# A three-stage perceiver kernel on one core: identity products ahead of the first rows, W transposed on TensorE, and four smaller moves

## The chip, the cores and the metric

The kernel runs on one core of one Trainium2 chip. The metric is the device time of an execution in microseconds (us), lower is better. A profiled execution gives, beside its own time, a trace of every engine: TensorE (PE; its weight loads are listed apart as PEld), VectorE (DVE), ScalarE (ACT), GpSimd (POOL) and SyncE (SP), which here only starts DMAs.

## What is computed

Three residual stages on x, 8 x 64 tokens of width 512, all in float32. The first stage attends over a context of 8 x 1601 rows; its matrix W is used twice, once on the queries and once, transposed, on the result:

```python
def _L0_xattn_ref(proj_p, proj_q, W, b):
    trans_q = jnp.einsum('bqh,oh->bqo', proj_q, W) + b
    att_weights = jnp.einsum('bph,bqh->bpq', proj_p, trans_q)
    att_norm = jax.nn.softmax(att_weights, axis=-1)
    att_vec = jnp.einsum('bpq,bqh->bph', att_norm, proj_q)
    return jax.nn.relu(jnp.einsum('bph,oh->bpo', att_vec, W) + b)

x = x + _L0_xattn_ref(_layernorm(x, axis=-1), ctx_1024, L0_xattn_W, L0_xattn_b)
x = x + _L0_attn_ref(_layernorm(x, axis=-1), ...)
x = x + _L0_ffn_ref(_layernorm(x, axis=-1), ...)
```

The second stage is a transformer block with causal linear attention of 16 heads (features elu(x proj) + 1) and a gelu MLP of width 2048. The third is a mixture of 8 experts (gated MLPs of width 1024), of which each token takes its best 2.

## The kernel before

The 512 tokens are NT = 4 tiles of 128, and 512 columns are KC = 4 chunks of 128. Every engine executes its instructions in the order in which the program writes them; nothing is rearranged.

**Start.** SP loads x and W (w_sb, L113), then everything else in one list (`stream`, `order`, `issue_to`): context keys (ctxT), context rows (ctx), the small inputs and the later weights. Large items go into a ring of RING = 12 buffers, and an item is started only when the buffer that it will take has been read. A second copy of W, transposed on the host (xw_t), is in that list behind the first context rows and lands in w_t. On POOL five areas inside v_sb are cleared first (L122); small vectors are loaded into every 32nd row of them later. Then the identity (ident) and other constants are made.

The rows of x are normalized by VectorE and ACT, two tiles at a time, and turned by `turn_p` (4 PE transposes and one ACT copy per tile). The queries times W, `pw_half`, are made in 2 halves of the tokens x 4 chunks; each is 4 accumulated matmuls of 256 columns. An f32 matmul is two records in the trace, a transpose is one.

**Context stage.** For each tile t, `key_group(t, g)` makes scores for a quarter g of the keys, `softmax` and `turn_scores` follow, `weigh(t, g)` multiplies by a third g of the rows, `turn_av` and `attended` multiply by w_t. `add_and_normalize(t)` is a chain of VectorE and ACT steps over the result, which ends in hn; `turn_h(t)` turns hn with 4 PE transposes and 4 VectorE steps into h_t; and `values(t, n)` multiplies h_t by half n of wv. For the last tile the order on PE is values(2, 0), values(2, 1), turn_h(3), values(3, 0), values(3, 1).

**Linear attention.** Eight pairs of heads j pass through `linear`, `features`, `products` and `attend_j`; the last step of `attend_j(j)` is a VectorE chain that ends in a_t. `output(t, js)` accumulates the output products of tile t over j. After `attend_j(7)`, PE has output(2) for j = 0 to 3, and then the j = 6 and 7 of tiles 0 and 1, the second of which needs the last a_t. `join` and `normal` follow on VectorE and ACT, and `turn_h2` on PE.

**Router and experts.** After the MLP the tokens are ranked by expert; "counts" is a small matmul into a bank of the tag "mm", read by VectorE. The PSUM pool is then closed and a new one (pse) opened. `whole_tile` runs an expert on 128 gathered tokens: up products, gating, transposes, and `down` into one bank y of 128x512. `add_rows` scales y and adds it to the output in DRAM by an indirect DMA. For the last expert's tile ACT scales the left half of y and VectorE the right one.

PSUM has 8 banks of 128x512 f32; in the first pool four have the tag "mm" (`mm_bank`) and four "acc" (`acc_bank`).

Of the kernel before, what the change touches and what calls it, by code (L numbers as in the profile page):

```python
# [32 lines left out]
NE, FE = 8, 1024  # L33
NQ = 4
FQ = FE // NQ
R = P // NQ
REST = 3 * R
# [3 lines left out]
NBIG = 7  # L41
LN_EPS = 1e-5
RING = 12
AHEAD = 6


@with_exitstack
def perceiver_kernel(
# [5 lines left out]
    context_tail: bass.AP,  # L54
    context_last: bass.AP,
    xw: bass.AP,
    xw_t: bass.AP,
    xb: bass.AP,
    wq: bass.AP,
    wk: bass.AP,  # L60
# [11 lines left out]
    nc = tc.nc  # L72
# [11 lines left out]
    def mm_bank(name):  # L84
        return ps.tile([P, 512], F32, tag="mm", name=name)
# [21 lines left out]
    h_t = la.tile([P, KC, B * S], F32, name="h_t")  # L107
# [10 lines left out]
    half = H * DH // 2  # L118
    last_in = [v_sb[:, 2, :half], v_sb[:, 2, half:], v_sb[:, 3, half:], v_sb[:, 1, half:]]
    xb_in = v_sb[:, 0, :D]  # L120
    for rows in [xb_in, *last_in]:
        nc.gpsimd.memset(rows, 0.0)  # L122
    col = const.tile([P, COLS], F32, name="col")

    streamed, order, issued = {}, [], [0]
# [2 lines left out]
    def stream(key, src):  # L128
        order.append((key, src))
# [20 lines left out]
        stream_keys(1, g)  # L150
    for t in range(NT):
        stream_rows(t, 0)
        if t == 0:
            stream("xw_t", xw_t)
        stream_keys(t + 1, 2)
        stream_rows(t, 1)
        stream_keys(t + 1, 3)
        stream_rows(t, 2)
        stream(("tail", t), context_tail[t])
        for g in range(2):  # L160
            stream_keys(t + 2, g)
        if t == NT - 2:
            for n in range(2):
                stream(("wv", n), wv[n])
# [16 lines left out]
    places_of = {"xb": xb_in[0:P:32, :], "col": col, "xw_t": w_t}  # L181
    places_of.update({("last", t): last_in[t][0:P:32, :] for t in range(NT)})

    def in_ring(key):
# [36 lines left out]

    ident = const.tile([P, P], F32, name="ident")
    make_identity(nc, ident)
    eps = const.tile([P, 1], F32, name="eps")
    nc.gpsimd.memset(eps, LN_EPS)
    warm0 = const.tile([P, 1], F32, name="warm0")
# [140 lines left out]
    def turn_p(t):  # L367
        bank = mm_bank(f"tr_p_{t}")
        for c in range(KC):
            nc.tensor.transpose(bank[:, c * P : (c + 1) * P], pn[:, t, c * P : (c + 1) * P], ident)  # L370
        nc.scalar.copy(p_t[:, :, t * P : (t + 1) * P], bank.rearrange("p (c q) -> p c q", c=KC))
# [4 lines left out]
    def pw_half(half, hc):  # L376
        cols = slice(half * 2 * P, (half + 1) * 2 * P)
        bank = mm_bank(f"pw_{half}_{hc}")
        for oc in range(KC):
            nc.tensor.matmul(  # L380
                bank[:, : 2 * P],
                w_sb[:, oc, hc * P : (hc + 1) * P],
                p_t[:, oc, cols],
                start=(oc == 0),
                stop=(oc == KC - 1),
            )
        nc.scalar.copy(pw_t[:, hc, cols], bank[:, : 2 * P])
# [3 lines left out]
    for t in range(0, NT, 2):  # L391
        of = [statistics(xs[:, t + h, :], f"p_{t + h}") for h in range(2)]
        for h in range(2):
            normalize(pn[:, t + h, :], xs[:, t + h, :], *of[h], f"p_{t + h}")
        if t == 0:
            turn_p(0)
            turn_p(1)
    pw_half(0, 0)
    pw_half(0, 1)
    turn_p(2)  # L400
    turn_p(3)
    pw_half(0, 2)
# [146 lines left out]
    def turn_h(t):  # L549
        bank = mm_bank(f"tr_h_{t}")  # L550
        for c in range(KC):
            nc.tensor.transpose(bank[:, c * P : (c + 1) * P], hns[t][:, c * P : (c + 1) * P], ident)
        for c in range(KC):
            nc.vector.tensor_scalar(  # L554
                h_t[:, c, t * P : (t + 1) * P],
                bank[:, c * P : (c + 1) * P],
                g1_c[:, c : c + 1],
                beta1_c[:, c : c + 1],
                ALU.mult,
                ALU.add,  # L560
            )

    def values(t, n):
        wv_n = need("wv", n)
        bank = mm_bank(f"v_{n}_{t}")
        for c in range(KC):
            nc.tensor.matmul(  # L567
                bank, h_t[:, c, t * P : (t + 1) * P], wv_n[:, c, :], start=(c == 0), stop=(c == KC - 1)
            )
        nc.scalar.copy(v_sb[:, t, n * 512 : (n + 1) * 512], bank)  # L570
# [49 lines left out]
            values(t - 2, 1)  # L620
        attended(t)
    add_and_normalize(NT - 1)
    for n in range(2):
        values(NT - 2, n)
    turn_h(NT - 1)
    for n in range(2):
        values(NT - 1, n)
    done(("wv", 0), ("wv", 1))
# [6 lines left out]
    if True:  # L635
        a_t = la1.tile([P, H * DH // P, B * S], F32, name="a_t")

        nj = H * DH // P
# [115 lines left out]
        def output(t, js):  # L754
            if t not in wo_banks:
                wo_banks[t] = (mm_bank if t < 2 else acc_bank)(f"wo_{t}")
            for j in js:
                nc.tensor.matmul(  # L758
                    wo_banks[t],
                    a_t[:, j, t * P : (t + 1) * P],  # L760
                    wo_r[j // 4][:, j % 4, :],
                    start=(j == 0),
                    stop=(j == nj - 1),
                )
# [8 lines left out]
        products(nj - 1)  # L773
        output(1, range(nj - 2))
        attend_j(nj - 1)
        output(2, range(nj // 2))
        for t in range(2):
            output(t, [nj - 2, nj - 1])

# [34 lines left out]
        of = join(0), join(1)  # L814
        for t in range(2):
            normal(t, *of[t])
        output(2, range(nj // 2, nj))
        of = join(2)
        output(3, range(nj // 2))
        normal(2, *of)  # L820
# [234 lines left out]
    t = NT - 1  # L1055
# [85 lines left out]
    if True:  # L1141
# [5 lines left out]
        def y_bank(side, name):  # L1147
            return pse.tile([P, 512], F32, tag=f"y{side}", name=name)
# [64 lines left out]
        def add_rows(key, y, n, side, by_vector=False):  # L1213

            _, dst, gate = slots[key]
            y_sb = moe2.tile([P, D], F32, tag=f"ysb{side}", bufs=2 - side, name=f"y_sb_{key[0]}_{key[1]}")
            if key == (NE - 1, 0):
                nc.scalar.activation(y_sb[:n, : D // 2], y[:n, : D // 2], AF.Copy, scale=gate[:n, :])
                nc.vector.tensor_scalar(y_sb[:n, D // 2 :], y[:n, D // 2 :], gate[:n, :], None, ALU.mult)
            elif by_vector:  # L1220
                nc.vector.tensor_scalar(y_sb[:n, :], y[:n, :], gate[:n, :], None, ALU.mult)
            else:
                nc.scalar.activation(y_sb[:n, :], y[:n, :], AF.Copy, scale=gate[:n, :])  # L1223
            nc.gpsimd.indirect_dma_start(  # L1224
                out=out,
                out_offset=bass.IndirectOffsetOnAxis(ap=dst[:n, :], axis=0),
                in_=y_sb[:n, :],
                in_offset=None,
                bounds_check=B * S + P - 1,
                oob_is_err=True,  # L1230
                compute_op=ALU.add,
            )

        def whole_tile(key, up_of, down_of, between=lambda k: None, side=0):


            nm = f"{key[0]}_{key[1]}"
            xg_t = turned[key]

            def up(q):  # L1240
                bank = side_bank(side, f"up_{nm}_{q}")
                for c in range(KC):
                    nc.tensor.matmul(  # L1243
                        bank, xg_t[c], up_of[q][:, c, :], start=(c == 0), stop=(c == KC - 1)
                    )
                return gated(side, bank, f"{nm}_{q}")

            def down(q, h_t):
                w = down_of[q // 2]
                for j in range(2):  # L1250
                    nc.tensor.matmul(  # L1251
                        y, h_t[:, j, :], w[:, 2 * (q % 2) + j, :], start=(q + j == 0), stop=(q + j == NQ)
                    )
# [12 lines left out]
            between(1)  # L1266
            h_t3 = hidden_t(side, hid3, f"{nm}_3")
            down(2, h_t2)
            between(2)
            down(3, h_t3)  # L1270
            add_rows(key, y, P, side)

        def group(e, up_of, down_of):


            nm = f"{e}_1"
# [5 lines left out]
            hid, h_t = [], {}  # L1282
# [7 lines left out]
            for h in range(2):  # L1290

                bank = side_bank(1, f"up_{nm}_1") if h else y_bank(1, f"up_{nm}_0")
                for c in range(KC):
# [3 lines left out]
                    for q in range(NQ):  # L1297
# [4 lines left out]
                            start=(c == 0),  # L1302
# [33 lines left out]
            add_rows((e, 1), y, R, 1)  # L1336

        def three_groups(e, up_of, down_of):

            nm = f"{e}_1"  # L1340
# [69 lines left out]
            add_rows((e, 1), y, REST, 1, by_vector=True)  # L1410

        if True:

# [225 lines left out]
    "ctx_tail",  # L1639
    "ctx_last",  # L1640
    "L0_xattn_W",
    "L0_xattn_W_T",
    "L0_xattn_b",
    "L0_attn_wq",
    "L0_attn_wk",
# [82 lines left out]
```

## Time and profile before

| what | us | from |
|---|---|---|
| median of 3 runs (650.0 to 650.8) | 650.71 | times |
| the profiled execution | 647.66 | times |
| its span, first to last instruction | 645.5 | page, head |
| first PE instruction | 7.45 | PE's timeline |
| start of the scores | 28.0 | chain of waits |
| last context rows weighed, tile 3 | 150.5 | chain of waits |
| last of v | 177.4 | chain of waits |
| start of the MLP's hidden products | 285.9 | PE's timeline |
| first expert product | 409.1 | PE's timeline |
| last y is scaled | 637.8 | timeline |

The page divides the span into 40 slices of 16.1 us. Its row for the DMA queues reads:

```profile
GB/s 345 405 414 422 423 425 421 427 426 422 193 80 47 86 2 131 1 131 0 130 52 79 70 96 95 134 95 348 114 375 54 200 206 338 173 367 188 274 18 16
```

The first ten numbers are the start and the context stage; after them the loads have room. In the lists of waits a row names the instruction that waited, its line, what it waited for, the total, how often and the longest. In a timeline a row has its start, its length, engine, line, operation, result <- operands, the shape and the number of instructions merged; in brackets stands the idle time before it and what ended that. Rows of PE overlap a little, because the end of a matmul is modelled.

### The profile page before, as it was taken

To read this page: it belongs to the slowest core of one execution; us is meant where nothing else is said; L and a number is where in the kernel's file an instruction comes from. 1 tells how busy PE (TensorE), PEld (TensorE's weight loads), DVE (VectorE), ACT (ScalarE), POOL (GpSimd) and SP (SyncE) were. 2 spreads that over 40 slices of the span, in tenths; PEclk is the share of its full clock that TensorE was granted. 3 is DMA by queue.
4 is the path that set the end of the run, shared out by engine and by line. 5 is a ranking of instruction groups with operands and counts; after the bars stand their busy time and mean duration, and the time that the engine had idled before them with its cause. 6 is when DMAs were issued, how large, how long until landed. Compare 5 with 4: busy or idle time off the path is not lost.

```text
span 645.5 us, 7558 instructions
## 1 busy us (share of the span) xinstructions
PE 620.4 (96%) x2956; PEld 292.7 (45%) x2956; DVE 185.5 (29%) x450; ACT 127.8 (20%) x245; POOL 64.6 (10%) x87
## 2 busy tenths in 40 slices
PE   4999999999999999999999999999999999999994
PEld 3743434344444444455444447544443344444441
DVE  5011333332316888660000035511311211011100
ACT  2241222220132123031101211311111111111110
POOL 4000000000000000050000002250102012103000
PEclk9999999999999999999999999999999999999998
DMA  8999999999421203030312222339392549496611
GB/s 345 405 414 422 423 425 421 427 426 422 193 80 47 86 2 131 1 131 0 130 52 79 70 96 95 134 95 348 114 375 54 200 206 338 173 367 188 274 18 16
DMA packets 23755, 132.70 MB, mean 206 GB/s; under 512 B 4084, under 2 KB 4084, under 8 KB 12184
## 3 DMA queue, kind: packets, MB, share of 16 engines
q1 hardware_dynamic: 19352, 123.37, 48.0%
q0 software_dynamic: 3248, 7.58, 5.3%
q10 hardware_dynamic: 1104, 1.07, 0.5%
q8 instruction: 33, 0.54, 0.3%
q14 instruction: 18, 0.15, 0.1%
HBM read 127.10 MB, written 4.91 MB: 204 GB/s over the span
## 4 chain that ended last, share of the span: by engine, by line
PE 50%; DMA 23%; issue 22%; DVE 2%; POOL 1%; POOLq 1%; ACT 0%; SPq 0%; ACTq 0%
DMA out_dram<-y_sb,dst_late 11%; DMA ctx<-in_ctx_dram 11%; PE hid L839 8%; PE mlp L860 8%; PE wk L647 4%; PE wq L647 4%; PE v L567 4%; PE wo L758 4%; PE sc L442 3%; PE av L503 3%; PE pw L380 3%; PE pr_wq L663 1%; PE xo L537 1%; PE qk L689 1%; POOL xg L1166 1%
## 5 line engine op out<-in xcount | busy, mean ns | idle before, releaser
L1243 PE MATMUL up<-e_up,xgT 128*128 128x512 f32 x224 | 100.2, 595 | 2.3 <-PEq L1569 1.4
L1243 PEld LDWEIGHTS up<-e_up,xgT 128*128 128x128 f32 x224 | 40.9, 190 | 49.9 <-issue 48.1
L1251 PE MATMUL y<-e_wo,hidT 128*128 128x512 f32 x128 | 60.8, 598 | 0.0
L839 PE MATMUL hid<-v_sb,w 128*128 128x512 f32 (+2 forms) x144 | 56.6, 545 | 0.0
L1202 DVE TENSOR_TENSOR mid<-up,act 128x256 f32<-128x256 f32 x35 | 14.9, 425 | 132.0 <-ACT act L1200 132.0
L860 PE MATMUL mlp<-w,hid_sb 128*128 128x512 f32 x112 | 51.0, 597 | 0.0
L503 PE MATMUL av<-ctx,eT 128*64 128x512 f32 x192 | 46.6, 597 | 0.7 <-DMA ctx<-in_ctx_dram 0.6
L442 PE MATMUL sc<-ctxT,pw_t 128*64 128x401 f32 (+1 forms) x256 | 46.2, 501 | 0.0
L839 PEld LDWEIGHTS hid<-v_sb,w 128*128 128x128 f32 x144 | 26.2, 190 | 29.1 <-issue 27.3
L1224 POOL DMA_INDIRECT out_dram<-y_sb,dst_late x12 | 18.3, 1524 | 174.3 <-ACT y_sb L1223 55.7
L1200 ACT ACTIVATE act<-up 128x256 f32<-128x256 f32 x35 | 13.4, 384 | 107.2 <-PE up L1243 97.4
L854 POOL TENSOR_TENSOR xin<-xin,b_bc 128x512 f32<-128x512 f32 x4 | 5.1, 1265 | 272.6 <-DVE rstd_h L796 268.4
L1251 PEld LDWEIGHTS y<-e_wo,hidT 128*128 128x128 f32 x128 | 22.5, 190 | 19.9 <-issue 19.6
L860 PEld LDWEIGHTS mlp<-w,hid_sb 128*128 128x128 f32 x112 | 20.7, 190 | 23.5 <-issue 23.4
L442 PEld LDWEIGHTS sc<-ctxT,pw_t 128*64 128x64 f32 x256 | 19.5, 136 | 25.6 <-issue 24.3
L758 PE MATMUL wo<-wo,a_t 128*128 128x512 f32 x64 | 29.1, 600 | 0.5 <-DVE a_t L734 0.5
L647 PE MATMUL wk<-h_t,wk 128*128 128x512 f32 x64 | 29.5, 604 | 0.0
L647 PE MATMUL wq<-h_t,wq 128*128 128x512 f32 x64 | 29.4, 602 | 0.0
L567 PE MATMUL v<-wv,h_t 128*128 128x512 f32 x64 | 28.7, 596 | 0.6 <-DVE h_t L554 0.6
L908 DVE TENSOR_TENSOR xs<-mlp,xs 128x512 f32<-128x512 f32 x3 | 2.1, 692 | 86.6 <-PE mlp L860 86.6
L732 DVE RECIPROCAL rden<-rden 128x512 f32<-128x512 f32 x8 | 26.8, 3353 | 0.3
L503 PEld LDWEIGHTS av<-ctx,eT 128*64 128x64 f32 x192 | 13.7, 136 | 26.8 <-issue 23.2
(266 smaller groups left out, 651.4 us busy)
## 6 DMA issues: line engine op xcount, KB each, us to landing
e_up<-in_L_ffn_up_dram SPq DMA_DIRECT2D x32, 1024.0 KB, 8.0
ctx<-in_ctx_dram SPq DMA_DIRECT2D x24, 1024.0 KB, 17.2
ctxT<-in_ctx_T_dram SPq DMA_DIRECT2D x24, 802.0 KB, 14.8
e_wo<-in_L_ffn_wo_dram SPq DMA_DIRECT2D x16, 1024.0 KB, 9.6
w<-in_L_attn_w_dram SPq DMA_DIRECT2D x8, 1024.0 KB, 4.7
ctxT<-in_ctx_T_dram SPq DMA_DIRECT2D x8, 796.0 KB, 17.5
wv<-in_L_attn_wv_dram SPq DMA_DIRECT2D x2, 1024.0 KB, 16.6
wq<-in_L_attn_wq_dram SPq DMA_DIRECT2D x2, 1024.0 KB, 17.8
```

The source lines that it names most:

```text
L380: nc.tensor.matmul(bank[:, : 2 * P], w_sb[:, oc, hc * P : (hc + 1) * P], p_t[:, oc, cols], start=(oc == 0), stop=(oc == KC - 1),)
L442: nc.tensor.matmul(sc[h * S : (h + 1) * S, :width], pw_t[:, c, (2 * t + h) * S : (2 * t + h + 1) * S], keys[h][:, c, :], start=(c == 0), s ...
L503: nc.tensor.matmul(av[h * S : (h + 1) * S, :], e_t[:, 4 * g + j, h * S : (h + 1) * S], rows[h][:, j, :], start=(g == 0 and j == 0), stop=F ...
L567: nc.tensor.matmul(bank, h_t[:, c, t * P : (t + 1) * P], wv_n[:, c, :], start=(c == 0), stop=(c == KC - 1))
L647: nc.tensor.matmul(bank, w[:, c, (j % 4) * P : (j % 4 + 1) * P], h_t[:, c, :], start=(c == 0), stop=(c == KC - 1),)
L732: nc.vector.reciprocal(rden, rden)
L758: nc.tensor.matmul(wo_banks[t], a_t[:, j, t * P : (t + 1) * P], wo_r[j // 4][:, j % 4, :], start=(j == 0), stop=(j == nj - 1),)
L839: nc.tensor.matmul(hid_banks[f][:, tokens], w[:, c, (f % 4) * P : (f % 4 + 1) * P], h2_t[:, c, tokens], start=(c == 0), stop=(c == KC - 1),)
L860: nc.tensor.matmul(acc[t], hid[:, t * P : (t + 1) * P], need("w2", f // 4)[:, f % 4, :], start=(f == 0), stop=(f == FF // P - 1),)
L1224: nc.gpsimd.indirect_dma_start(out=out, out_offset=bass.IndirectOffsetOnAxis(ap=dst[:n, :], axis=0), in_=y_sb[:n, :], in_offset=None, boun ...
L1243: nc.tensor.matmul(bank, xg_t[c], up_of[q][:, c, :], start=(c == 0), stop=(c == KC - 1))
L1251: nc.tensor.matmul(y, h_t[:, j, :], w[:, 2 * (q % 2) + j, :], start=(q + j == 0), stop=(q + j == NQ))
```

## The change

Six edits, in the order of the program:

1. The load of xw_t and the host's transpose are gone. The five clears on POOL move behind the identity.
2. NIDLE = 12 products of the identity with itself go to PE as soon as the identity is there, into a bank of the tag "acc" which nobody reads.
3. After the first two `turn_p`, PE turns W itself with 16 transposes of 128x128 into four "acc" banks; VectorE copies these to w_t, behind the first normalizations and ahead of the shuffle of xb.
4. `turn_h(3)` is issued inside values(2, 1), ahead of its last matmul.
5. output(2) takes j = 4 ahead of the last products of tiles 0 and 1 instead of behind them.
6. "counts" takes an "acc" bank. The last tile's y becomes two banks, each with 256 columns used; `down` makes its two matmuls for one bank and then for the other, and ACT and VectorE each read one.

```diff
+NIDLE = 12
...
-    for rows in [xb_in, *last_in]:
-        nc.gpsimd.memset(rows, 0.0)
...
-        if t == 0:
-            stream("xw_t", xw_t)
...
     make_identity(nc, ident)
+
+    idle_bank = acc_bank("idle")
+    for _ in range(NIDLE):
+        nc.tensor.matmul(idle_bank[:, :P], ident, ident, start=True, stop=True)
+    for rows in [xb_in, *last_in]:
+        nc.gpsimd.memset(rows, 0.0)
...
             turn_p(0)
             turn_p(1)
+
+            w_banks = [acc_bank(f"w_t_{hc}") for hc in range(KC)]
+            for hc in range(KC):
+                for oc in range(KC):
+                    nc.tensor.transpose(
+                        w_banks[hc][:, oc * P : (oc + 1) * P], w_sb[:, oc, hc * P : (hc + 1) * P], ident
+                    )
     pw_half(0, 0)
     pw_half(0, 1)
+    for hc in range(KC):
+        nc.vector.tensor_copy(w_t[:, hc, :], w_banks[hc])
...
-    def values(t, n):
+    def values(t, n, among=lambda: None):
...
         for c in range(KC):
+            if c == KC - 1:
+                among()
...
-    for n in range(2):
-        values(NT - 2, n)
-    turn_h(NT - 1)
+    values(NT - 2, 0)
+    values(NT - 2, 1, lambda: turn_h(NT - 1))
...
-        output(2, range(nj // 2))
+        output(2, range(nj // 2 + 1))
...
-        output(2, range(nj // 2, nj))
+        output(2, range(nj // 2 + 1, nj))
...
-    bank = mm_bank("counts")
+
+    bank = acc_bank("counts")
...
-            if key == (NE - 1, 0):
-                nc.scalar.activation(y_sb[:n, : D // 2], y[:n, : D // 2], AF.Copy, scale=gate[:n, :])
-                nc.vector.tensor_scalar(y_sb[:n, D // 2 :], y[:n, D // 2 :], gate[:n, :], None, ALU.mult)
+            if len(y) == 2:
+                nc.scalar.activation(y_sb[:n, : D // 2], y[0][:n, : D // 2], AF.Copy, scale=gate[:n, :])
+                nc.vector.tensor_scalar(y_sb[:n, D // 2 :], y[1][:n, : D // 2], gate[:n, :], None, ALU.mult)
...
+                width = D // len(y)
+                for n, bank in enumerate(y):
+                    for j in range(2):
+                        nc.tensor.matmul(
+                            bank[:, :width],
+                            h_t[:, j, :],
+                            w[:, 2 * (q % 2) + j, n * width : (n + 1) * width],
...
-            y = y_bank(side, f"y_{nm}")
+            y = [y_bank(side, f"y_{nm}")]
+            if key == (NE - 1, 0):
+
+                y.append(y_bank("w", f"y_{nm}_1"))
...
-    inputs["L0_xattn_W_T"] = _np.asarray(inputs["L0_xattn_W"]).T
```

More of the change, by code (lines that the diff above doesn't have):

```diff
@@ L56, in perceiver_kernel @@
     xw: bass.AP,
-    xw_t: bass.AP,
     xb: bass.AP,
@@ L179, in perceiver_kernel @@
     place = {key: i for i, (key, _) in enumerate(order)}
-    places_of = {"xb": xb_in[0:P:32, :], "col": col, "xw_t": w_t}
+    places_of = {"xb": xb_in[0:P:32, :], "col": col}
     places_of.update({("last", t): last_in[t][0:P:32, :] for t in range(NT)})
@@ L1216, in add_rows @@
             y_sb = moe2.tile([P, D], F32, tag=f"ysb{side}", bufs=2 - side, name=f"y_sb_{key[0]}_{key[1]}")
-            if key == (NE - 1, 0):
-                nc.scalar.activation(y_sb[:n, : D // 2], y[:n, : D // 2], AF.Copy, scale=gate[:n, :])
-                nc.vector.tensor_scalar(y_sb[:n, D // 2 :], y[:n, D // 2 :], gate[:n, :], None, ALU.mult)
+            if len(y) == 2:
+                nc.scalar.activation(y_sb[:n, : D // 2], y[0][:n, : D // 2], AF.Copy, scale=gate[:n, :])
+                nc.vector.tensor_scalar(y_sb[:n, D // 2 :], y[1][:n, : D // 2], gate[:n, :], None, ALU.mult)
             elif by_vector:
+                (y,) = y
                 nc.vector.tensor_scalar(y_sb[:n, :], y[:n, :], gate[:n, :], None, ALU.mult)
             else:
+                (y,) = y
                 nc.scalar.activation(y_sb[:n, :], y[:n, :], AF.Copy, scale=gate[:n, :])
@@ L1249, in down @@
                 w = down_of[q // 2]
[L1250 to L1253, printed above, removed]
+                width = D // len(y)
[5 more added lines that the diff above has]
+                            w[:, 2 * (q % 2) + j, n * width : (n + 1) * width],
+                            start=(q + j == 0),
+                            stop=(q + j == NQ),
+                        )
             hid0 = up(0)
@@ L1335, in group @@
                 )
-            add_rows((e, 1), y, R, 1)
+            add_rows((e, 1), [y], R, 1)
         def three_groups(e, up_of, down_of):
@@ L1409, in three_groups @@
                 folded(g, n)
-            add_rows((e, 1), y, REST, 1, by_vector=True)
+            add_rows((e, 1), [y], REST, 1, by_vector=True)
         if True:
@@ L1641 @@
     "L0_xattn_W",
-    "L0_xattn_W_T",
     "L0_xattn_b",
@@ L1705, in by_cols @@
         return _np.asarray(w).reshape(KC, P, -1, 512).transpose(2, 1, 0, 3)
-    for name in ("L0_xattn_W", "L0_xattn_W_T"):
-        inputs[name] = by_rows(inputs[name])[0]
+    inputs["L0_xattn_W"] = by_rows(inputs["L0_xattn_W"])[0]
     for name in ("L0_attn_wq", "L0_attn_wk", "L0_attn_wv", "L0_attn_w1"):
```

## The prediction

> **What bounds the kernel now.** I read the busy shares first, then TensorE's waits, then its timeline at the few places where it stands still. The page's first row says that TensorE (PE) is the kernel:
>
> ```profile
> PE 620.4 (96%) x2956; PEld 292.7 (45%) x2956; DVE 185.5 (29%) x450; ACT 127.8 (20%) x245; POOL 64.6 (10%) x87
> ```
>
> A change pays only where PE stands still or runs slowly. The list of PE's waits (total us, times, longest) names the places:
>
> ```profile
> PE tr_p L370 <- DVE rstd_p L362: 7.4, 1, 7.4
> ...
> PE pw L380 <- ACT h_t L371: 0.7, 1, 0.7
> PE v L567 <- DVE h_t L554: 0.6, 1, 0.6
> PE av L503 <- DMA ctx<-in_ctx_dram: 0.6, 2, 0.3
> PE wo L758 <- DVE a_t L734: 0.5, 1, 0.5
> ```
>
> Four of these are touched by the change. What the list can't show is slow work, so PE's timeline of the first 28 us comes next (start, us, instruction):
>
> ```profile
> 7.45 1.94 PE L370 MATMUL tr_p<-ident,xin 128*128 128x128 f32 x8 [7.45 <-DVE rstd_p L362]
> 10.06 6.72 PE L380 MATMUL pw<-h_t,w_sb 128*128 128x256 f32 x16 [0.68 <-ACT h_t L371]
> 16.62 1.04 PE L370 MATMUL tr_p<-ident,xin 128*128 128x128 f32 x8
> 17.49 10.53 PE L380 MATMUL pw<-h_t,w_sb 128*128 128x256 f32 x48
> ```
>
> The same products take 0.42 us each at first and 0.216 later (the chain of waits has 10.36 us for the 48); the transposes fall from 0.22 to 0.109 (0.87 for 8). PE works at half rate until about 16.3, though the granted clock reads 1.00 throughout: that column doesn't show this gate.
>
> Last, the DMA of the context stage, from the table of windows (the last columns are granted clock, DMA share, GB/s) and PE's timeline:
>
> ```profile
> 31.00:32.00 1.00, 1.00 (x8) 0.43 (x6) 0.00 (x0) 0.54 (x1) 0.00 (x0) 1.00 1.14 376
> 32.00:33.00 1.00, 1.00 (x8) 0.43 (x6) 0.00 (x0) 0.00 (x0) 0.00 (x0) 1.00 0.84 232
> ...
> 90.34 3.65 PE L503 MATMUL av<-ctx,eT 128*64 128x512 f32 x14 [0.29 <-DMA ctx<-in_ctx_dram]
> ...
> 121.25 3.65 PE L503 MATMUL av<-ctx,eT 128*64 128x512 f32 x14 [0.29 <-DMA ctx<-in_ctx_dram]
> ```
>
> From 34 to 160 us the queues move 419 to 427 GB/s without a dip, and PE stops for 0.29 us at the same point of each round, 30.9 us apart. DMA's round is 30.9 and PE's 30.6: **DMA sets the pace until 121 us**, with PE just behind. After that PE sets it. So what PE gains before 28 us survives only as far as DMA gains too.
>
> **The first rows.** The row clears (five memsets, 0.81 to 3.18) now follow the identity, which took 0.56 us on POOL (3.14 to 3.70): it is ready at 1.37 instead of 3.70, and the clears end at 3.74. POOL's sum is unchanged, so everything behind them keeps its time. The load of xb waits for its clear, up to 0.56 us longer, and on SP six key loads stand behind it; the queues then hold some 3.0 MB (x, W, two key blocks, less what moved), 7 us of work, so nothing runs dry.
>
> The 12 identity products are plain f32 products, two records each: 24 x 0.215 = 5.2 us at half rate, about 1.45 to 6.65, before the first normalized rows at 7.45: free. If weight load and product did not overlap they would cost some 0.4 each (the shortest record is 379 ns), 9.6 us, and PE would reach the first transposes at 11.05, 3.6 late. The transposes of 7.45 have the same size and run 0.22 apart; I take 5.2.
>
> What they buy is the open gate. The row: in this trace it opened 8.9 us after the first transpose, 6.2 after the first product. [...]
>
> With an open gate: transposes of rows 0 and 1, 8 x 0.109, end at 8.32. W itself is the new wait: issued at 1.74, 7.1 us to landing, 8.84. Its 16 transposes run 8.9 to 10.65 (1.74), which covers the two ACT copies that cost 0.68. Then 16 x 0.216 = 3.46, 0.87 for rows 2 and 3 (normalized at 11.64), 48 x 0.216 = 10.37: the scores start at 25.35 instead of 28.02, **2.67 earlier**. Four copies of W's banks (0.69 each, the row of o_sb) stand on VectorE ahead of the bias sums, which end at about 18.5 instead of 15.9 and are read at 28 or later; w_t is first read at 70.8. Free, with 2.8 us at stake if that cover were gone.
>
> **The removed load.** 1,024 KB at 424 GB/s is 2.47 us less for everything behind it, from the second key blocks of tile 1 on. The dip above is the queue running dry because the ring waited for the first score group (30.89): 48 + 192 KB short, 0.57 us. Freed 2.7 earlier, it doesn't occur. DMA gains 3.04; PE's own path gains 2.67 + 0.71 (its three waits: 0.13 between 55 and 60, where the windows show it busy for 4.87 of 5.00, and 0.29 twice) = 3.38. The later one counts: **3.04** in this execution. The dip belongs to a late gate, and other executions may have opened it sooner, so for the median I take 2.8 (between 2.47 and 3.04).
>
> **v's last transposes.** They now precede the last two records of values(2, 1), 0.86 us of cover for a wait of 0.59. VectorE ends hn at 168.12, the transposes would start at 168.29: 0.17 to spare, at worst 0.1 lost. The four VectorE steps and ACT's copy keep their order. **0.59**.
>
> **The output product.** PE ends at 271.08 and a_t comes at 271.63. Two records (0.86) cover it: **0.55**. VectorE's joins start 0.31 later, and one product fewer stands before turn_h2(0), at 280.5 instead of 281.2; normal(1) ends at 278.8. Nothing is late.
>
> **The counts bank.** counts and the first up product have the same bank (0 in the program's list of allocations); VectorE read it until 409.03 and up(0) began at 409.13 after 0.51 of idling. Even if all of it goes, the gathered rows xg of expert 0's rest land at 429.50 whatever PE does (PE's weight load already waits 0.17 for them), so up to 0.5 becomes a wait there. **0**, at most 0.1.
>
> **The last tile's two banks.** Twice the records at half the width, 0.216 each, with 0.19 weight loads under them as in the pw rows: free. The tail now:
>
> ```profile
> 636.80 0.47 ACT L1218 ACTIVATE y_sb<-y,xg 128x256 f32<-128x256 f32 x1 [3.01 <-PE y L1251]
> 637.31 0.48 DVE L1219 TENSOR_SCALAR y_sb<-y,xg 128x256 f32<-128x256 f32 x1 [4.93 <-ACT y_sb L1218]
> 638.07 1.55 POOL L1224 DMA_INDIRECT out_dram<-y_sb,dst_late  x1 [20.76 <-DVE y_sb L1219]
> ```
>
> VectorE waits for ACT. With its own bank ready 0.86 before the end, ACT finishes under PE and VectorE starts at 636.80: **0.51**.
>
> **Sum.** 2.8 + 0.59 + 0.55 + 0 + 0.51 = 4.45 us (4.7 against the profiled 647.66, whose span is 645.5). The runs' median is 650.71, 3 us above the profiled one, with no stage to pin it on; I carry the difference over: 650.71 - 4.45 = **646.3**.
>
> **Rivals.**
> - *The gate opens only after W.* At half rate row transposes end at 9.39 and W's at 12.83, 2.8 later than pw starts now. Opening at 16.3, 8 products run slow and scores start at 29.3, 1.25 late. PE then leads: 1.25 - 0.71 - 1.65 (the three later gains) = -1.1: **649.6**. [...] Against: 5.2 us of products come first.
> [...]
> - *The identity products overrun* to 11.05, gate open: scores at 28.35, 0.33 late; -0.38 - 1.65 = **648.7**.
> - *The load's removal is not the gain:* if PE reached 28 us no earlier, DMA's 2.47 would yield only PE's 0.71.
>
> **How the numbers follow.** Forecast 0.62 (own range 645.2 to 647.3); gate after W 0.16; its worst 0.12; overrun 0.06; something not seen 0.04. A measurement of this kernel tells about 0.2%, 1.3 us, from no change. Faster: 0.62 + 0.06 + a third of the late gate + 0.01 = 0.74. Same: 0.11 of the late gate and 0.05 of its worst, 0.16. Slower: 0.10. The range, 645.0 to 650.4, leaves out the worst case and the tails.
>
> **What would show it.** Right: tr_p records 0.109 apart at 7.45, W's transposes ending near 10.7, scores near 25.4, no dip at 32, the third-rows wait at the first tile about 3 us earlier, no waits at v and wo, VectorE's last step at PE's end. Wrong: pw records 0.42 apart, a first transpose after 7.6, or PE gaps in the rounds longer than 0.4.

## The result, and the profile after

| | us | from |
|---|---|---|
| before, median of 6 runs (649.2 to 651.2) beside the changed kernel | 650.36 | times |
| after, median of 6 runs (645.3 to 646.2) | 646.0 | times |
| ratio | 0.9925, 95% interval 0.991 to 0.9941 | times |
| profiled execution of after, and its span | 646.23, 644.5 | times, page |

The total came out as forecast, 646.0 against 646.3. Several of its terms were wrong, which is what the rest of this text is about. A caution first: the profiled execution of before (647.66) lies below all six runs that stood beside after, and that of after is the slowest of its six. The two spans differ by 1.0 us, the medians by 4.4, so the two traces are compared stage by stage and not by their ends.

PE's timeline of the first 28 us after (start, us, instruction, in brackets the idle time before it):

```profile
1.44 5.49 PE L223 MATMUL idle<-ident 128*128 128x128 f32 x24 [1.44 <-POOL ident masks.py:199]
7.61 1.43 PE L372 MATMUL tr_p<-ident,xin 128*128 128x128 f32 x8 [0.67 <-DVE xin L365]
8.87 1.95 PE L404 MATMUL w_t<-ident,w_sb 128*128 128x128 f32 x16
10.65 3.62 PE L382 MATMUL pw<-h_t,w_sb 128*128 128x256 f32 x16
...
25.44 4.94 PE L453 MATMUL sc<-ctxT,pw_t 128*64 128x401 f32 x28
```

Nearly to the tenth the front that was forecast: products done before the first rows, W's transposes at full rate until 10.65, the first 16 pw records in 3.62 instead of 6.72, scores at 25.44 instead of 28.0. The first transpose of x comes at 7.61, just past the 7.6 that was named as a sign of being wrong, because VectorE's rows came late (PE stood idle for 0.67 before it); it cost nothing, since W's transposes still start at 8.87, earlier than in the six later traces that have the full-size products or idle_turns' transposes ahead of them (8.96 to 9.14). But PE's waits for the context rows, which were to stay under 0.4, grew (the same timeline, later):

```profile
57.46 3.65 PE L514 MATMUL av<-ctx,eT 128*64 128x512 f32 x14 [0.66 <-DMA ctx<-in_ctx_dram]
...
88.98 3.65 PE L514 MATMUL av<-ctx,eT 128*64 128x512 f32 x14 [0.93 <-DMA ctx<-in_ctx_dram]
...
119.83 3.65 PE L514 MATMUL av<-ctx,eT 128*64 128x512 f32 x14 [0.25 <-DMA ctx<-in_ctx_dram]
```

The third-rows restart of tile 2, at 121.25 before, stands at 119.83: of the 2.5 us gained at the scores only 1.4 is left, and the waits for DMA took the rest. A dip of the queues is a part of why. The table of windows after (length, busy time of PE, PEld, DVE, ACT and POOL, then granted clock, DMA share, GB/s):

```profile
24.00:26.00 2.00, 2.00 (x11) 1.32 (x12) 0.00 (x0) 0.56 (x2) 0.00 (x0) 1.00 1.00 338
26.00:28.00 2.00, 2.00 (x14) 0.86 (x12) 0.00 (x0) 0.00 (x0) 0.00 (x0) 1.00 1.01 363
28.00:30.00 2.00, 2.00 (x16) 0.83 (x12) 0.00 (x0) 0.60 (x1) 0.00 (x0) 1.00 0.98 324
30.00:32.00 2.00, 2.00 (x16) 0.83 (x14) 0.00 (x0) 0.60 (x1) 0.00 (x0) 1.00 1.00 388
```

The dip at 32 is gone, and a deeper one stands at 24 to 30 (the same windows of before have 373, 417 and 412). Summing GB/s by time up to 44 us, the queues had moved 16,908 KB before and 16,718 after, so some 0.45 us of the 2.47 that the removed load saved was given back. That would leave 2.0; where the other 0.6 went is not shown.

At the other end the two y banks do what was meant, and nothing comes of it (timeline of all engines):

```profile
634.94 0.47 ACT L1231 ACTIVATE y_sb<-y,xg 128x256 f32<-128x256 f32 x1 [2.17 <-PE y L1268]
635.80 0.48 DVE L1232 TENSOR_SCALAR y_sb<-y,xg 128x256 f32<-128x256 f32 x1 [4.45 <-PE y L1268]
637.06 1.55 POOL L1239 DMA_INDIRECT out_dram<-y_sb,dst_late  x1 [20.79 <-DVE y_sb L1232]
```

ACT's half is done early and VectorE starts when PE ends. But the scatter starts 0.78 us after VectorE's end (635.80 + 0.48), where it took 0.28 before. From the first product of the last expert to the scatter there are 23.06 us (614.00 to 637.06), and 23.03 before.

### The profile page after: what moved, and what is told of

Same layout as the page of the kernel before. It is cut to its first block, busy times and chain, and to the rows that moved or that the text cites. A ratio compares the mean times of both kernels' runs of the same rounds, so it can differ in the third digit from the quotient of the medians.

```text
span 644.5 us, 7676 instructions
## 1 busy us (share of the span) xinstructions
PE 623.7 (97%) x3012; PEld 299.9 (47%) x3012; DVE 187.8 (29%) x454; ACT 127.8 (20%) x245; POOL 64.1 (10%) x87
## 5 line engine op out<-in xcount | busy, mean ns | idle before, releaser
L1268 PE MATMUL y<-e_wo,hidT 128*128 128x512 f32 (+1 forms) x144 | 60.8, 550 | 0.0
L1268 PEld LDWEIGHTS y<-e_wo,hidT 128*128 128x128 f32 x144 | 25.5, 190 | 18.2 <-issue 17.2
```

Of the source, the lines that this page charges most:

```text
L1268: nc.tensor.matmul(bank[:, :width], h_t[:, j, :], w[:, 2 * (q % 2) + j, n * width : (n + 1) * width], start=(q + j == 0), stop=(q + j == NQ),)
```

## The experiments

The theory after the result: the first three edits are worth what DMA gains, PE's start being hidden, and the later edits are worth their PE gaps. The rivals: the open gate is the gain; the new tail costs what it saves; a part of the time lies elsewhere. All kernels compute the whole output. Each ratio is to runs of before on the same chip; these had medians of 648.3, 648.0 and, for the last kernel, 651.0, so ratios are compared and not times.

### before_again: before once more

> The kernel before, unchanged, for a second trace. Its profiled execution was 647.66 us, while its other executions have a median of 650.4. [...] Theory B (the difference lies behind the context stage): the start is as before within 0.3 us, and PE shows more idle time at places without a releaser ('issue', 'PEq') in the expert stage. A time near 650 with the same PE timeline up to 409 us speaks for B.

647.57 us, one run. Scores at 27.70, third rows of tile 2 at 121.15, first expert product at 409.01: within 0.3 us of the first trace of before in each stage. So the stage marks of before can be relied on to some 0.3 us until the experts. The chip was one on which before's median is 648.3 and not 650, so whether the 3 us lie behind the context stage was not decided.

### no_idle: after without the identity products

```diff
-NIDLE = 12
+NIDLE = 0
```

> The changed kernel without its 12 identity products; W is still turned on TensorE and not loaded. [...] If the removed load carries the front alone (rival): within 0.7 us of the changed kernel.

644.45 us, 0.9943 (0.993 to 0.9956). The expectation failed: the products were to open the gate and carry the front with it, and without them the kernel still gains, some 0.2% less than after_again below. PE's timeline shows the first surprise:

```profile
7.28 1.94 PE L372 MATMUL tr_p<-ident,xin 128*128 128x128 f32 x8 [7.28 <-DVE rstd_p L364]
9.01 2.71 PE L404 MATMUL w_t<-ident,w_sb 128*128 128x128 f32 x16
11.56 3.62 PE L382 MATMUL pw<-h_t,w_sb 128*128 128x256 f32 x16
```

W's 16 transposes took 2.71 us: at 0.22 and 0.109 us each that is 7 or 8 slow ones, then fast ones. The gate opened at about 10.7, 3.4 us after the first transpose and ahead of any product. (best_no_idle, the other kernel without the products, opened it 4.9 us after its first transpose.) **It opened with nothing but transposes run.** The scores start at 26.34, only 0.9 later than after, and by the third rows that is gone: 118.65, the earliest of all. Up to the first expert product (404.87) this kernel is 1.2 us *ahead* of after. So where does it lose? The second surprise is in the first expert:

```profile
428.03 1.02 PE L1322 MATMUL up<-e_up,xgT 128*32 128x256 f32 x10 [0.44 <-PEq L1594]
430.51 2.79 PE L1322 MATMUL up<-e_up,xgT 128*32 128x256 f32 x46 [1.46 <-issue]
```

Ten products after a branch (PEq, L1594) PE stands for 1.46 us with nothing in the profile to wait for. In after the 56 products are one row (of 3.60 us; 3.23 in after_again). This was followed up last, with best_tiny.

### keep_load: identity products, but W's transpose loaded as before

```diff
+            stream("xw_t", xw_t)
...
-            w_banks = [acc_bank(f"w_t_{hc}") for hc in range(KC)]
...
-        nc.vector.tensor_copy(w_t[:, hc, :], w_banks[hc])
```

> The changed kernel with the transposed W loaded from DRAM as before, and not turned on TensorE; the identity products stay. If DMA sets the pace of the context stage (the prediction): scores start near 24.0, but the third rows of each tile come when the DMA has them, the waits there grow to 1 to 2 us, and the gain of the front is 0.6 to 1.3 us instead of 2.8: about 647.5 to 648.5, 1.5 to 2.2 us slower than the changed kernel. If the gate alone carries the front (rival): as fast as the changed kernel or 1 us faster.

646.49 us, 0.9968 (0.9956 to 0.998). Slower than the changed kernel, as expected, but by more: 0.0048 in the ratio beside after_again below, some 3.1 us, where 1.5 to 2.2 was expected. PE starts the scores at 24.19, earlier than any other kernel, and waits it all off (PE's timeline):

```profile
60.23 3.65 PE L508 MATMUL av<-ctx,eT 128*64 128x512 f32 x14 [1.31 <-DMA ctx<-in_ctx_dram]
...
121.96 3.65 PE L508 MATMUL av<-ctx,eT 128*64 128x512 f32 x14 [0.24 <-DMA ctx<-in_ctx_dram]
```

At 121.96 it is 0.7 behind before although it began 3.8 ahead. The open gate alone gains nothing in this stage: the removed load is the gain. Not all of the 3.1 us is the load, though: the stretch from the first expert's first product to the last expert's takes 206.3 us here and 205.1 in after_again, 1.2 less, though no expert's work differs.

### back_only: before with edits 4 to 6 alone

```diff
-    for n in range(2):
-        values(NT - 2, n)
-    turn_h(NT - 1)
+    values(NT - 2, 0)
+    values(NT - 2, 1, lambda: turn_h(NT - 1))
...
-        output(2, range(nj // 2))
+        output(2, range(nj // 2 + 1))
```

and the banks of counts and of the last y as in after.

> The kernel before with edits 4, 5 and 6 alone: v's last transposes, the output product, the counts bank, the two y banks. The prediction's sum for these is 0.59 + 0.55 + 0 + 0.51 = 1.65 us, a ratio of 0.9975 to before. If the waits only move to the next late thing: under 0.5 us, ratio over 0.999. In this kernel counts is in a bank of the second four, so up(0) may lose its 0.51 us of idling; the gathered rows should then take it back at the first xgt transposes.

647.17 us, 0.9976 (0.9967 to 0.9985). The total fits, the parts don't. PE's timeline at the output products, of before and then of back_only:

```profile
266.52 4.56 PE L758 MATMUL wo<-wo,a_t 128*128 128x512 f32 x10
271.63 9.71 PE L758 MATMUL wo<-wo,a_t 128*128 128x512 f32 x22 [0.55 <-DVE a_t L734]
281.18 1.04 PE L802 MATMUL tr_h<-ident,v_sb 128*128 128x128 f32 x8
```

```profile
265.49 14.00 PE L759 MATMUL wo<-wo,a_t 128*128 128x512 f32 x32
279.33 1.04 PE L803 MATMUL tr_h<-ident,v_sb 128*128 128x128 f32 x8
```

From the first wo product to the turn that follows, 13.84 us, and 14.66 before. The step gained 0.82, not the 0.55 in brackets there: a matmul's end is modelled late (the rows overlap), so the true gap is longer than the bracket says. (At 0.43 each, the ten records from 266.52 fill PE until 270.81, which is 0.82 before 271.63.) The v step is alike: 15.00 from 162.28 to wq before, 14.18 here, again 0.82 for a bracket of 0.59. And the tail gained nothing: 23.06 from the last expert's first product to the scatter. 1.64 in place of 1.65, by two errors that cancel. The span of this trace is only 1.0 below before's, for the stretch between the first products of the first and the last expert is 0.8 longer (206.7 against 205.9). One thing more was expected here: counts no longer shares the up product's bank, so that product might lose its 0.51 of idling. It kept it (407.28, in brackets 0.51).

### after_again, and idle_turns: after once more, and with transposes for the products

```diff
-NIDLE = 12
+NIDLE = 24
...
-        nc.tensor.matmul(idle_bank[:, :P], ident, ident, start=True, stop=True)
+        nc.tensor.transpose(idle_bank[:, :P], ident, ident)
```

> The changed kernel, unchanged, beside the other kernels of this call. From its first measurement: ratio 0.9925 to before, within 0.991 to 0.994. Its trace says how much of the DMA's late third rows (0.66, 0.93 and 0.25 us in the first one) is chance: if that was chance, the third rows of tile 2 come near 118.6, as without the identity products, instead of 119.8.

> The changed kernel with 24 transposes of the identity in place of its 12 products: as many records, as long. [...]

after_again 643.13 us, 0.992 (0.9906 to 0.9933); idle_turns 642.83, 0.9921 (0.9905 to 0.9936). The same. idle_turns has the transposes of x in 1.38, W's in 1.97 and the scores at 25.60, after_again has 1.37, 1.97 and 25.64: here 24 transposes open the gate as 24 product records do.

### swap_y: VectorE takes the first half of the last y, ACT the second

```diff
-                nc.scalar.activation(y_sb[:n, : D // 2], y[0][:n, : D // 2], AF.Copy, scale=gate[:n, :])
-                nc.vector.tensor_scalar(y_sb[:n, D // 2 :], y[1][:n, : D // 2], gate[:n, :], None, ALU.mult)
+                nc.vector.tensor_scalar(y_sb[:n, : D // 2], y[0][:n, : D // 2], gate[:n, :], None, ALU.mult)
+                nc.scalar.activation(y_sb[:n, D // 2 :], y[1][:n, : D // 2], AF.Copy, scale=gate[:n, :])
```

The reading behind it: the scatter must wait for two engines. In the program's list it carries the wait for ACT itself, and a separate instruction ahead of it in POOL's queue carries the wait for VectorE. The chain of waits of after shows this (start, us, what):

```profile
635.80 0.49 DVE y_sb L1232
636.30 0.03 POOLq L1239
636.33 0.51 issue
636.83 1.77 POOLq L1745
```

After VectorE's end there is the separate wait, then 0.51 us until the scatter's own. If VectorE is the early one, that 0.5 passes beside ACT's work.

> The changed kernel with the two halves of the last y exchanged between the engines: VectorE scales the first bank and ACT the second. In the changed kernel the DMA that adds the rows starts 0.78 us after VectorE's end instead of 0.28 as before, because its own wait is for ACT, and VectorE's end is waited for by an instruction of its own ahead of it in POOL's queue. If that is the cause: the DMA now starts 0.28 after ACT's end, 1.0 us after the last product instead of 1.5, and the time falls by 0.5 us, a ratio 0.0008 lower than the changed kernel's. If POOL needs this time whatever ends last (rival): 1.5 us after the last product, no gain.

642.28 us, 0.991 (0.9897 to 0.9924). The timeline of all engines:

```profile
631.54 0.48 DVE L1231 TENSOR_SCALAR y_sb<-y,xg 128x256 f32<-128x256 f32 x1 [3.59 <-PE y L1268]
632.41 0.47 ACT L1232 ACTIVATE y_sb<-y,xg 128x256 f32<-128x256 f32 x1 [3.03 <-PE y L1268]
633.16 1.55 POOL L1239 DMA_INDIRECT out_dram<-y_sb,dst_late  x1 [20.28 <-ACT y_sb L1232]
```

0.28 us from ACT's end to the scatter, as before had after VectorE's. From the last expert's first product (610.61) it is 22.55 us where before and after have 23.03 and 23.06; the three kernels with this order that follow have 22.55 too. The 0.5 us that edit 6 was to bring comes with this order; the ratio's interval is too wide to show it, the stretch in the trace is not.

### counts_mm: counts in a bank of the tag "mm" again

```diff
-    bank = acc_bank("counts")
+    bank = mm_bank("counts")
```

> The changed kernel with counts in a bank of the tag 'mm' again. In the changed kernel the tag 'acc' is used first and so lies in banks 0 to 3, and counts is in bank 0 again, as the first up product is; with 'mm' it is in bank 4. If the shared bank is the cause of the 0.51 us before up(0): the first up product starts 0.5 us sooner after the last first_rows product (1.2 us instead of 1.7). By the prediction the gathered rows then take it back: PE waits at the second xgt transposes of expert 0, and the time is the same within 0.2 us. Rival: the gain stays, and the time falls by 0.5 us.

642.76 us, 0.9921 (0.9904 to 0.9939), no difference. The timeline of all engines at the first up product:

```profile
404.94 0.15 DVE L1125 COPY count<-counts 128x8 f32<-128x8 f32 x1
...
405.20 1.10 PE L1258 MATMUL up<-e_up,xgT_first 128*128 128x512 f32 x2 [0.51 <-issue]
```

In after the identity products had taken the tag "acc" first and so got banks 0 to 3; counts went to bank 0 again. Here counts is in bank 4, the up product in bank 0, and the 0.51 stays. So the shared bank is not the cause. In the program's list the product waits for VectorE's copy of counts in both, and here it starts 0.11 after that copy's end; the PSUM pool is closed and reopened between them. That this is the cause is the author's reading of the list and not shown: a reopened pool with the copy taken ahead wasn't tried.

### small_late: the five small loads behind tile 1's first key blocks

In after SP's waits for landings at the start are each for the load eight places before: ahead of the tenth, eleventh and twelfth load it waits 0.7, 2.2 and 1.9 us for the second, the third (w_sb) and the fourth, ahead of the 18th to 20th 2.9, 1.6 and 1.8 us for the tenth to twelfth. Four loads of 8 KB (the last context rows) and one of 32 KB take places among blocks of 800 to 1,024 KB; behind them fewer large blocks are in flight, and a key block lands 6.1 us after its issue (the median of four in after), where key blocks from 28 us on take 14 to 18 (medians).

```diff
+    for g in range(2):
+        stream_keys(1, g)
     for t in range(NT):
         stream(("last", t), context_last[t])
     stream("col", columns)
-    for g in range(2):
-        stream_keys(1, g)
```

> The changed kernel with one more edit: the five small loads (four last context rows, the columns) come behind the first key blocks of tile 1 in the load list instead of ahead of them. Every load on SP waits for the one eight places before it, so the small loads hold places in flight; in the traces of the changed kernel the key blocks behind them land 6.1 us after their issue (some 3 of them in flight) against 17.5 later, and DMA moves only 230 to 390 GB/s between 24 and 32 us. If the places are the cause: the key blocks are issued by 20 us instead of 22 to 27, the rate stays over 400 until 29, the third rows of tile 2 come 0.7 to 1.3 us earlier than in the changed kernel (119.8, 120.3; so near 118.6), and the time falls by 0.5 to 1 us, a ratio near 0.991. If the small loads are slow in themselves or the dip has another cause (rival): the dip only moves, and nothing is gained.

642.22 us, 0.991 (0.9895 to 0.9926). Its windows, with columns as above:

```profile
26.00:28.00 2.00, 2.00 (x16) 0.83 (x14) 0.00 (x0) 0.03 (x1) 0.00 (x0) 1.00 1.00 411
28.00:30.00 2.00, 2.00 (x15) 0.83 (x13) 0.00 (x0) 0.60 (x1) 0.00 (x0) 1.00 1.03 423
...
34.00:36.00 2.00, 2.00 (x14) 0.86 (x12) 0.00 (x0) 0.54 (x1) 0.00 (x0) 1.00 0.97 373
36.00:38.00 2.00, 2.00 (x14) 0.85 (x12) 0.75 (x1) 1.36 (x2) 0.00 (x0) 1.00 0.95 349
```

The dip moved with the small loads, from 24 to 30 to 34 to 38. So the small loads make the dip, whose place follows them. That it became smaller is not shown: small_late had moved 16,828 KB by 44 us and best, which has the same order of loads, 16,768, while the kernels with the small loads early spread from 16,576 (after_again, swap_y) to 17,046 (no_idle). Nor is it settled whether moving them pays: the third rows restart at 118.75 here and at 119.23 in best; after, after_again, swap_y, idle_turns and counts_mm have 118.96 to 120.30, and no_idle 118.65.

### best, best_no_idle and best_tiny: what are the identity products worth?

best is small_late with swap_y. best_no_idle is best with NIDLE = 0. best_tiny keeps the products in place and number, and takes the work out of them:

```diff
-        nc.tensor.matmul(idle_bank[:, :P], ident, ident, start=True, stop=True)
+        nc.tensor.matmul(idle_bank[:1, :1], ident[:, :1], ident[:, :1], start=True, stop=True)
```

> The small loads late and the halves of the last y exchanged, together. 0.5 us below the kernel with the small loads late, through the last DMA's start 0.75 us after ACT begins its half; ratio 0.990 to 0.991. If one of the two gave nothing, the ratio of the other alone.

> The same without the identity products. [...] If DMA still sets the pace of the context stage: 0.3 us or less is lost, since PE has 0.3 us of waits per tile to give. [...]

> best with its twelve identity products kept in place and number but cut to one column of weights and one column of data, so that they end by about 3 us and cannot hold TensorE busy until the first rows come; the program list of TensorE stays as long as that of best. Theory one, the products are worth 1.9 us because the front starts at full rate: W's transposes run at half rate for a part again, the scores start near 27.1 as in best_no_idle instead of 25.56, and the time is that of best_no_idle, 0.9946 of before. Theory two, the front's 1.6 us are hidden by the context loads, and what best_no_idle loses is the stall of 1.72 us after ten products of the first small tile (431.08), which hangs on how many instructions lie ahead: the scores start near 27.1 too, but there is no stall over 1 us between 428 and 434, the stretch from the first up-projection to the first of the second expert is about 30.9 as in best and not 33.2, and the time is that of best, 0.991. A stall that comes whenever the front is slow, for whatever reason, would give theory one's time with theory two's place.

best 642.31 us, 0.9912 (0.9896 to 0.9928), no better than swap_y or small_late alone; the three can't be told apart. best_no_idle 644.2, 0.9946 (0.993 to 0.9961), more lost than was expected. best_tiny 644.44 beside 650.99 for before, **0.9904 (0.989 to 0.9919)**: the time of best, and clear of best_no_idle's interval. PE's timeline of best_tiny:

```profile
1.45 0.74 PE L223 MATMUL idle<-ident 128*1 128x1 f32 x24 [1.45 <-POOL ident masks.py:199]
...
9.00 2.52 PE L404 MATMUL w_t<-ident,w_sb 128*128 128x128 f32 x16
...
26.14 4.27 PE L453 MATMUL sc<-ctxT,pw_t 128*64 128x401 f32 x24
...
428.20 3.23 PE L1322 MATMUL up<-e_up,xgT 128*32 128x256 f32 x56 [0.44 <-issue]
```

The products end at 2.2, W's transposes are slow for a part again, the scores come 0.6 later than in best (not at 27.1, as expected, since the gate opened by 10.3), and it costs nothing. In the first expert the 56 products run without a stop. In best_no_idle they don't:

```profile
428.35 1.02 PE L1322 MATMUL up<-e_up,xgT 128*32 128x256 f32 x10 [0.44 <-PEq L1594]
431.08 2.79 PE L1322 MATMUL up<-e_up,xgT 128*32 128x256 f32 x46 [1.72 <-issue]
```

| kernel | scores | third rows, tile 2 | first expert product | to the second expert's first |
|---|---|---|---|---|
| best | 25.56 | 119.23 | 405.45 | 30.86 |
| best_tiny | 26.14 | 118.82 | 405.05 | 30.86 |
| best_no_idle | 27.15 | 118.96 | 405.19 | 33.17 |
| no_idle | 26.34 | 118.65 | 404.87 | 32.91 |

So theory two holds. The 1.3 to 1.9 us that the kernels without the products lose are the stop in the first expert (2.0 to 2.3 longer there). It goes with the instructions that lie ahead of it in PE's program, not with the work that they do: best_tiny has 48 more than best_no_idle (24 records, each with its weight load), which take 0.74 us, and no stop. What stops PE is not shown. Two traces with other counts have a shorter stop at another product. In before and in back_only the same row of 56 breaks after 28 products, for 0.21 and 0.34 us; no_idle has W's 16 transposes more ahead of it, 32 instructions, and breaks 18 products, 36 instructions, sooner. That is nearly the same place in the program, though before_again shows no stop there at all.

## Why the prediction was right, and where it was wrong

The sum was right in part by luck: two terms were too large, two too small, and a gain that was not foreseen made up the rest. Measured in the traces, those of the changed kernels, all but after's own, from a chip where before takes 648:

| term | forecast | measured |
|---|---|---|
| the front, seen at the third rows of tile 2 | 2.8 | 1.7 (0.9 to 2.2 in after, after_again, swap_y, idle_turns, counts_mm) |
| v's last transposes | 0.59 | 0.82 |
| the output product | 0.55 | 0.82 |
| the counts bank | 0 | 0 |
| the last y | 0.51 | 0 |
| first product of the first expert to that of the last | none | 0.9 (205.9 in both traces of before; 204.8 to 205.1 in after_again, swap_y, idle_turns, counts_mm) |
| sum | 4.45 | 4.2, beside 4.4 and 5.2 between the medians |

After's own trace adds up otherwise: 1.4 at the front, twice 0.82, nothing at the end, and the last row of the table with its sign turned, 207.9 us (406.07 to 614.00), 2.0 more than before. That is the 1.0 us between the two spans.

- **The front on PE: right.** 24 records in 5.49 instead of 5.2, transposes to 10.65, scores at 25.44 for a forecast of 25.35. That 5.2 us of products would open the gate, on which the 2.67 and so the 2.8 rest, was the author's estimate: in before's trace full rate came 6.2 us after the first product. In after the 24 records took 5.49 us, and W's transposes, 16 in 1.95, ran at full rate from the first. W's landing as the new wait shows in five later traces (0.29 to 0.56 us) and not in after's own.
- **"Freed 2.7 earlier, it doesn't occur": true of the dip at 32, wrong of the sum.** This is the largest step that failed. The dip was put down to the ring waiting for the first score group, and DMA was to gain 0.57 there beside the 2.47 of the removed load. A second cause was not seen: the small loads that take places in SP's queue, and with them a dip at 24 to 30 us. DMA's gain came to 1.4 in after's own trace and 0.9 to 2.2 in the others, in place of 3.04. That DMA sets the pace there was right, and keep_load shows it: early scores alone gave nothing.
- **"PE's own path gains 2.67 + 0.71": too small.** From the first score to the third rows of tile 2, before takes 93.3 us (27.95 to 121.25), best_no_idle 91.8 (27.15 to 118.96). So PE had at least 1.5 us of waits to give and not the 0.71 of the brackets, each of which falls short by some 0.25, as at v and wo below. The rival *the load's removal is not the gain* is thereby too low as well: best_no_idle starts its scores only 0.8 earlier than before and is 2.3 earlier at the third rows.
- **"What they buy is the open gate": true, and worth nothing.** The forecast weighed it against a gate that opens at 16.3, with scores at 29.3. Without the products it opened at 10.7 and 12.2, with scores at 26.3 and 27.15 (no_idle, best_no_idle), and the context loads hide that much: best_tiny, no_idle and best_no_idle lose 0.6 to 1.6 us at the scores and nothing at the third rows.
- **A gate that opens late: wrong.** *The gate opens only after W* had 0.16 of the chance and "its worst" 0.12. In no_idle the gate opened 3.4 us after the first transpose with nothing else run, in best_no_idle 4.9 us after it, in best_tiny, where the tiny products end 5.0 us ahead of the rows, 3.1. All three opened it while PE turned W, by 12.2 at the latest, and after had it open before: the late gate, on which both chances rest, is in no run that turns W.
- **v and wo: the mechanism right, the size off.** The bracket of a PE row is measured from a modelled end. 0.59 and 0.55 were true gaps of 0.82 each.
- **The last y: wrong.** VectorE does start at PE's end, 0.5 earlier. The scatter's second wait, a separate instruction with 0.5 us behind it, took that back; swap_y got it again.
- **The counts bank: the value right, the reason wrong.** It isn't the same bank, as back_only and counts_mm show. That the closing of the pool is the cause is the author's reading and not shown.
- **The signs of being wrong** were only half of use. Waits of 0.66 and 0.93 in the rounds were beyond the 0.4 named, and pointed to DMA; but before_again has 0.45 at the same place and back_only 0.90 and 0.54, with the front unchanged, so such a wait doesn't tell the kernels apart.
- **The difference carried over.** The median of before stands 3 us above its profiled time, and the forecast carried that over with no stage to pin it on. In after's trace PE stops at two places where it doesn't in after_again's (PE's timeline):

```profile
531.18 0.64 PE L1339 MATMUL yq<-e_wo,hidT 128*32 128x256 f32 x8 [0.76 <-issue]
...
586.24 0.64 PE L1339 MATMUL yq<-e_wo,hidT 128*32 128x256 f32 x8 [0.82 <-issue]
```

best_tiny, on a chip where before took 651.0, has waits of 0.72 and 0.75 at the same two places; the traces from the chips where before took 648 have none that long. Most of the difference between these chips lies among the experts: from the first expert's first product to the last one's, after takes 207.9 us and after_again 205.1, which is 2.8 of the 2.9 between their medians, and best_tiny takes 208.0 where best takes 205.3. Why is open. Before's trace, with 205.9, looks like those of the faster chips; that it came from such a one is likely, and the record doesn't say. The 0.9 us in the expert stage are read from two traces before and four after; back_only, with 206.7, and keep_load, with 206.3, have it the other way. That the place of instructions makes this difference too is a guess of the author's and not shown.

## What to carry to other kernels

Here DMA's round took 30.9 us and PE's 30.6, and scores 3.8 us earlier on PE alone had gained nothing at the third rows of tile 2 (keep_load). So where two resources run that close, weigh each edit against the slower one, and test it with an edit that takes the work out and leaves the instructions in. In this kernel 12 tiny products at the start of PE's program, there or not, changed the time of the first expert by 2.3 us (30.86 and 33.17), about as much as the best single edit here; a "useless" edit can win or lose for that alone. A wait that joins two engines need not be symmetric: here the scatter came 0.28 us after the late engine's end when that engine had the wait on the scatter itself, and 0.78 when it had the separate one.

## What was not expected of the hardware

- PE came to full rate on transposes alone: 3.4 us after the first of them in no_idle and 4.9 in best_no_idle, f32 transposes of 128x128 falling from 0.22 to 0.109 us. The granted-clock column reads 1.00 throughout. In the two traces of before the gate opened at 16.3 and 15.95, 6 us after the first product, though half-rate transposes had begun at 7.45 and 7.35; a gap of 0.68 us lay between. In back_only, with the same front and the same gap, it opened at 14.1. (15.95 and 14.1 are reckoned from the records in windows of 2 us.)
- A stop of PE of 1.46 and 1.72 us without any releaser, ten products behind a branch, which is there without, and gone with, 12 tiny products (24 records) at the start of the program, 426 us earlier.
- An indirect DMA on POOL that waits for two engines starts 0.28 us after ACT's end when ACT is the last (swap_y) and 0.78 after VectorE's when that is (after).
- Five loads of 64 KB in all, ahead of large ones, go with a fall of the queues' rate from some 420 to between 324 and 388 GB/s for several us in after. That they do it by holding places and not by their bytes is read from the order of issue and from the dip moving with them; the places were not changed by themselves.
